# A four-layer graph network on one core: the attention's first tiles made in layer 2, its outer heads summed in float32, and layer 3's chunks run further ahead

## The chip, the cores and the metric

The program runs on one core of one Trainium2 chip. The metric is the device time of one execution in microseconds, as the median of several runs. The core's engines run beside each other and meet only at semaphores: TensorE (PE) multiplies matrices from SBUF into PSUM, PEld is its loading of weights, VectorE is called DVE, ScalarE ACT, GpSimd POOL, and SyncE (SP) issues most of the DMA transfers. Each engine executes its own queue in order, so an instruction that waits holds up all that stands behind it on that engine.

## The reference, cut to what matters

Four layers work on 2708 nodes with 512 features each and one adjacency matrix. Each layer normalizes its rows, takes the positive part, aggregates over neighbors and adds the result to its input. Layer 2 is the attention that the change is about (8 heads of 64 columns):

```python
Wh = jnp.einsum('nd,hdo->hno', x, W)
f1 = jnp.einsum('hno,ho->hn', Wh, a1)
f2 = jnp.einsum('hno,ho->hn', Wh, a2)
e = jax.nn.leaky_relu(f1[:, :, None] + f2[:, None, :], negative_slope=ALPHA)
e = jnp.where(adj[None, :, :] > 0, e, NEG_INF)
attention = jax.nn.softmax(e, axis=-1)
h_prime = jnp.einsum('hnm,hmo->hno', attention, Wh)
out = jax.nn.elu(h_prime)
```

Layer 3 averages the neighbors, multiplies by two weight matrices (fused with a third at the kernel's start) and takes the positive part.

## The kernel before, in words

Rows are cut into 22 chunks of 126 (the last has 62). Line numbers are those of the kernel before.

*Around the attention.* Layer 2 starts with a pass over its 22 chunks (`staged`, with one function per stage and a lag for each): load a chunk of x, normalize, transpose on PE (`hT_ps`), multiply by the attention's weights on PE (`wh_ps`, L182), copy, and write the product to the DRAM array `whd`. Beside it DVE and POOL form the two sums f1 and f2 of each head, PE transposes f1 into rows (`row2`, L728), which go to the DRAM array `rT`; the last four rows are done inside the attention.

*The attention* (from L829) never forms a softmax over raw scores. Since exp(leaky_relu(a + b)) is the larger of two products of factors of a and of b, a tile of weights needs one DVE instruction (`make`, L895): the larger of a broadcast row `rb` (factor of the node that asks) and a column `ec` (factor of the neighbor), times the 0/1 pattern of the adjacency `vT`. The rest of the neighbor's factor, `ef`, is multiplied into the neighbor's rows of `wh` by ACT (`scale`, L868, giving `whs`). The work goes unit by unit. A unit is a head over all 2708 nodes; the first and the last head are each cut into two units, over 1384 and 1324 nodes, so there are ten units: 2 halves, 6 full heads, 2 halves. Each unit takes 22 steps, one for each chunk of neighbors, 220 steps in all.

In each step `multiply` (L919) sends the tile through PE twice. The `av` product, with 64 columns of `whs`, works in quarters of the array's columns: four matmuls of 32 columns each run side by side on four parts of the tile. A float32 matmul appears in the trace as two passes. The `sums` product is the softmax's denominator. In 9 of 22 steps it is a float32 product with a further 32 columns of `whs`, made by a second ACT instruction (L870). In the 13 others, listed in `BY_SIDE`, ACT compares the tile against a threshold by a steep sigmoid (`compare`, L880, result `b` in bf16), and PE multiplies `b` in bf16 by the neighbor's factors split into three bf16 parts (`parts`); this gives a part of the denominator, and the remainder needs, for each node, the sum of the neighbor's factors over its neighbors. That is `count_neighbors`: for each of the 13 chunks, ACT turns the adjacency pattern into bf16 in four quarters (L978, `x<-vT`, in the five buffers named `x` that also hold chunks of x) and PE multiplies them by the parts (L983, `adj_sums`). Before, it stands behind steps 66 to 78, the first 13 of head 2 (unit 3, as heads and units count from 0). The parts are split by POOL in `exps2`.

At a unit's end ACT copies the sums out of PSUM (`evict`, L958) and SP writes them to the DRAM arrays `avT` and `sumT`. A list, `plan`, says behind which step each such thing is issued; a scheduler then places the instructions on the engines, and may place one ahead of its position in the program where it finds nothing that holds it. Up to four weight tiles exist at once (`TILES`), so DVE can be three steps ahead of PE. [...]

*After the attention* layer 3 passes over the chunks again. For each: load its part of `avT` and `sumT` (`load3`), transpose and divide on PE and DVE (`turn3`), apply elu on POOL, ACT and DVE (`elu3`), normalize, save x, transpose (`hT_ps`), and multiply by two weights (`nb_ps`, `self_ps`, L182). For the first chunks some of this is placed in the attention's last steps. Then comes layer 3's aggregation, 132 groups of products with the adjacency (L330), whose PE time ends the kernel.

Of the kernel before, what the change touches and what calls it, by code (L numbers as in the profile page):

```python
# [20 lines left out]
P = 128  # L21

R = 126
# [21 lines left out]
def fast_layers(  # L45
# [59 lines left out]
    KMAX = max(sizes)  # L105
    EARLY = NC // 2
# [152 lines left out]
    def load_x(src, c, name="x", pool=None, bufs=5, twice=False):  # L259
        n = rows(c)  # L260
        t = (pool or common).tile([P, D], F32, name=name, bufs=bufs)
        if twice and c == NC - 1:
            nc.gpsimd.memset(t[:R], 0.0)
            move(nc.sync, t[TAIL : TAIL + n, :], src[c * R : c * R + n, :])
        move(nc.sync, t[:n], src[c * R : c * R + n, :])
        return t
# [383 lines left out]
    l2 = ctx.enter_context(ExitStack())  # L650
    cp = l2.enter_context(tc.tile_pool(name="l2", bufs=1, side="right", reuse_waits="tile"))
# [5 lines left out]
    ef = cp.tile([R, NC, H], F32, name="ef")  # L657
    ec = cp.tile([R, NC, H], F32, name="ec")
    eb = cp.tile([R, NC, H], F32, name="eb")
    parts = cp.tile([R, NC * H * 8 + S], BF16, name="parts")  # L660
    nc.gpsimd.memset(parts, 0.0)
    parts_of = parts[:, : NC * H * 8].rearrange("p (m h k) -> p m h k", h=H, k=8)
    parts2 = cp.tile([R, NC, 3 * H], BF16, name="parts2")
    one6 = cp.tile([R, S], F32, name="one6")
    nc.gpsimd.memset(one6, 0.0)
    nc.gpsimd.memset(one6[:, 6:7], 1.0)
    row = {}

    def load_row1(h, lo, hi):

        if lo == 0:
            row[h] = cp.tile([R, N], F32, name="rb", bufs=2)
        src = rT[h : h + 1, lo:hi]
        nc.sync.dma_start(
            row[h][:, lo:hi],
            bass.AP(tensor=src.tensor, offset=src.offset, ap=[[0, R], [1, hi - lo]]),
        )

    def exp_row(h, lo, hi):
        t = row[h][:, lo:hi]  # L680
        nc.scalar.activation(t, t, AF.Exp, scale=1.0 - SLOPE2)

# [43 lines left out]
    def row2(c):  # L726
        pf = ps.tile([P, R], F32, name="f_ps", tag="ps")
        nc.tensor.transpose(pf[:H], f12[:R, c, :H], ident[:R, :R])  # L728
        r = cp.tile([H, R], F32, name="row", bufs=2)
# [3 lines left out]
    def exps2(cs):  # L733
        nc.scalar.activation(ef[:, cs], f12[:R, cs, H:], AF.Exp)
        nc.scalar.activation(ec[:, cs], f12[:R, cs, H:], AF.Exp, scale=SLOPE2 - 1.0)
        nc.gpsimd.tensor_scalar(eb[:, cs], ec[:, cs], -STEEP * ABOVE, None, op0=ALU.mult)
        size = cs.stop - cs.start
        rest = cp.tile([R, EARLY, H], F32, name="rest")[:, :size]
        for i, e in enumerate((ef, ec)):
            if i:  # L740
                nc.gpsimd.tensor_tensor(rest, ec[:, cs], ef[:, cs], ALU.mult)
                e = rest
            else:
                e = ef[:, cs]
            for k in range(3):
                part = parts_of[:, cs, :, 3 * i + k]
                nc.gpsimd.tensor_copy(part, e)
                if k < 2:
                    nc.gpsimd.tensor_tensor(rest, e, part, ALU.subtract)
                    e = rest  # L750
        nc.gpsimd.tensor_copy(
            parts2[:, cs].rearrange("p m (h k) -> p m h k", k=3), parts_of[:, cs, :, 3:6]
        )
# [4 lines left out]
    def rows2(c):  # L758
        if c < LATE:
            row2(c)  # L760
        if c == EARLY - 1:
            load_row1(*units[0])
        if c == NC - 4:
            exps2(slice(0, EARLY))
            exp_row(*units[0])

# [6 lines left out]

    ws = load_weight(weights, fused[0], "wfs", tag="w")
    wn = load_weight(weights, fused[1], "wfn", tag="w")
# [3 lines left out]
    e3 = e3_ctx.enter_context(tc.tile_pool(name="e3", bufs=2, reuse_waits="tile"))  # L779
    er = e3.tile([R, NC, H], F32, name="er", bufs=1)  # L780
    kept3 = {}
# [58 lines left out]
    with ExitStack() as stack:  # L840
        at = stack.enter_context(tc.tile_pool(name="att", bufs=1, reuse_waits="tile"))
        weight, wh, whs, acc, sides = {}, {}, {}, {}, {}
        steps = [(u, m) for u in range(len(units)) for m in range(NC)]


        GROUP = 3

        def load_wh(s):
            u, m = steps[s]
            h = units[u][0]  # L850
            t = at.tile([R, GROUP, O], F32, name="wh", bufs=3)
            k = min(GROUP, NC - 1 - m)
            if k > 0:
                src = whd[m * R : (m + k) * R, h * O : (h + 1) * O]
                nc.sync.dma_start(t[:, :k], src.rearrange("(k p) o -> p k o", p=R))
            if k < GROUP and m + k == NC - 1:
                src = whd[(NC - 1) * R :, h * O : (h + 1) * O]
                nc.sync.dma_start(t[:last_rows, k], src)
            for j in range(GROUP):
                wh[u, m + j] = t[:, j]  # L860

        def scale(s):

            u, m = steps[s]
            h, q = units[u][0], rows(m)
            t = at.tile([R, O + S], F32, name="whs", bufs=4)
            by = ef[:q, m, h : h + 1]
            nc.scalar.activation(t[:q, :O], wh.pop((u, m))[:q], AF.Copy, scale=by)  # L868
            if m not in BY_SIDE:
                nc.scalar.activation(t[:q, O:], one6[:q], AF.Copy, scale=by)  # L870
            whs[s] = t

        def compare(s):

            u, m = steps[s]
            h, lo, hi = units[u]
            q = rows(m)
            if m in BY_SIDE:
                b = at.tile([R, N], BF16, name="b", bufs=2)
                nc.scalar.activation(  # L880
                    b[:q, : hi - lo],
                    weight[s][:q, : hi - lo],
                    AF.Sigmoid,
                    bias=eb[:q, m, h : h + 1],
                    scale=STEEP,
                )
                sides[s] = b

        def make(s):
            u, m = steps[s]  # L890
            h, lo, hi = units[u]
            q = rows(m)
            g, k = where[m]
            t = at.tile([R, N], F32, name="t2", bufs=TILES)
            nc.vector.scalar_tensor_tensor(  # L895
                t[:q, : hi - lo],
                row[h][:q, lo:hi],
                ec[:q, m, h : h + 1],
                vT[g][:q, k, lo:hi],
                op0=ALU.max,  # L900
                op1=ALU.mult,
            )
            weight[s] = t

        def pieces(w):

            k = -(-w // 512)
            cuts = [round(i * w / k) for i in range(k + 1)]
            return list(zip(cuts, cuts[1:]))

        def sizes_of(u):
            _, lo, hi = units[u]
            return (hi - lo) // 2, (hi - lo) // 4

        def four(out, size, operands, m):

            for p, (a, b) in zip(out, pieces(size)):
                for j, (lhsT, rhs, part) in enumerate(operands):
                    nc.tensor.matmul(  # L919
                        p[j * S : j * S + lhsT.shape[1], : b - a],  # L920
                        lhsT,
                        rhs[:, part * size + a : part * size + b],
                        start=(m == 0),
                        stop=(m == NC - 1),
                    )

        def multiply(s):
            u, m = steps[s]
            q = rows(m)
            half, quarter = sizes_of(u)  # L930
            if m == 0:
# [847 lines left out]
```

## Time and profile before

| | us |
|---|---|
| median of 3 runs (range) | 1877.04 (1876.25 to 1879.04) |
| the profiled execution | 1876.26 |
| its span, first to last instruction | 1874.1 |
| PE busy in the span | 1803.5 (96%) |
| DVE busy | 1302.2 (69%) |
| ACT busy | 900.5 (48%) |
| POOL busy | 234.5 (13%) |
| mean granted clock of TensorE | 0.984 of full |

The busy times of engines overlap. A matmul's end is modelled, so a full PE row says that PE had work issued all the time, not that it ran at its peak. In the profile's lines L is the line of the kernel, the arrow reads "output from inputs", x is a count, and the bracket at a timeline row's end gives the idle time of that engine ahead of it and what ended it.

First starts of the attention's units on PE, read from the trace: 901.2, 941.1 (head 0), 974.4, 1039.7, 1128.1, 1192.8, 1257.8, 1323.3 (heads 1 to 6), 1388.5, 1421.9 (head 7); the last `av` matmul starts at 1456.2, layer 3's first product at 1473.5, and its aggregation at 1646.4.

### The profile page before, as it was taken

The numbers are of one execution on the slowest core, as the hardware profiler recorded it, in microseconds if no ns is written. First come the engines' busy times: TensorE is split into PE (matmuls) and PEld (weight loads), VectorE is DVE, ScalarE is ACT, GpSimd is POOL, SyncE is SP. The second block draws the span as 40 slices with busy tenths as digits, with TensorE's granted clock in tenths as the row PEclk, the third lists the DMA queues.
The fourth block names the chain that finished last, engine by engine and source line by source line (L and its number), as shares of the span: only waits on it lengthen the run. The fifth ranks groups of instructions, "written<-read, shape, count | busy, mean of one in ns | idle before, by whom it ended". The sixth has DMA issues, their size and how long they took to land.

```text
span 1874.1 us, 30317 instructions
## 1 busy us (share of the span) xinstructions
PE 1803.5 (96%) x11670; PEld 1057.0 (56%) x11670; DVE 1302.2 (69%) x1944; ACT 900.5 (48%) x1533; POOL 234.5 (13%) x219
## 2 busy tenths in 40 slices
PE   8999999989999999989899999999999799999998
PEld 4555677654447887744344443444444455478886
DVE  4655888874444566566899879999999766524333
ACT  2555887862220000056786897777777666400000
POOL 0000111211110122157400000000000222100000
PEclk9999999999999999999899999999999899999999
DMA  6423555542222112143320221210211444203321
GB/s 216 129 84 93 161 157 149 146 123 66 72 72 76 45 54 74 53 147 102 95 65 11 58 55 44 59 54 17 58 32 46 119 137 138 87 31 93 106 68 43
DMA packets 126037, 161.00 MB, mean 86 GB/s; under 512 B 57406, under 2 KB 77994, under 8 KB 125002
## 3 DMA queue, kind: packets, MB, share of 16 engines
q1 hardware_dynamic: 106764, 123.51, 23.2%
q10 hardware_dynamic: 18544, 33.37, 5.3%
q0 software_dynamic: 576, 2.10, 0.4%
q8 instruction: 94, 1.54, 0.3%
q14 instruction: 59, 0.48, 0.1%
HBM read 111.34 MB, written 47.42 MB: 85 GB/s over the span
## 4 chain that ended last, share of the span: by engine, by line
PE 65%; DVE 12%; issue 5%; ACT 4%; DMA 3%; POOL 0%; SPq 0%; DVEq 0%; ACTq 0%; POOLq 0%
PE acc L330 25%; PE av L919 12%; PE nb_ps L182 8%; DVE t L895 7%; PE self_ps L182 4%; PE line_ps L182 4%; PE sums L919 4%; PE wh_ps L182 4%; DVE cum L428 3%; PE hT_ps L210 2%; DMA rb<-rT 1%; DMA ai<-in_adj 1%; ACT cum L443 1%; ACT b L880 1%; ACT x L978 1%
## 5 line engine op out<-in xcount | busy, mean ns | idle before, releaser
L895 DVE SCALAR_TENSOR_TENSOR t<-rb,ec,vT 126x2708 f32<-126x2708 f32 (+2 forms) x220 | 528.2, 2470 | 25.5 <-ACT b L880 12.5
L919 PE MATMUL av<-t,whs 126*32 126x451 f32 (+4 forms) x4576 | 443.7, 517 | 8.7 <-ACT whs L868 7.5
L330 PE MATMUL acc<-halves,kt 126*126 126x512 f32 x1848 | 430.4, 394 | 1.2 <-DVE kt L1133 1.1
L330 PEld LDWEIGHTS acc<-halves,kt 126*126 126x126 f32 x1848 | 343.8, 186 | 85.4 <-DVE kt L593 1.5
L880 ACT ACTIVATE b<-t,eb 126x2708 bf16<-126x2708 f32 (+5 forms) x130 | 272.6, 2097 | 41.0 <-DVE t L895 40.2
L919 PEld LDWEIGHTS av<-t,whs 126*32 126x32 f32 (+1 forms) x4576 | 167.7, 110 | 204.1 <-issue 161.1
L330 PE MATMUL acc<-halves,ar 126*126 126x512 f32 x924 | 254.9, 415 | 6.1 <-ACT vT L483 4.9
L330 PEld LDWEIGHTS acc<-halves,ar 126*126 126x126 f32 x924 | 164.5, 188 | 50.9 <-issue 9.2
L593 DVE SCALAR_TENSOR_TENSOR kt<-lastr,index,vT 126x504 fp32r<-126x504 int16 (+1 forms) x132 | 105.0, 804 | 82.8 <-PE acc L330 82.8
L191 ACT ACTIVATE ln_rs<-ln_mv,eps 126x1 f32<-126x1 f32 x88 | 25.3, 293 | 276.9 <-DVE ln_mv L189 271.2
L1133 DVE CAST kt<-vT 126x504 fp32r<-126x504 int8 (+1 forms) x132 | 52.7, 400 | 140.8 <-PE acc L330 140.8
L428 DVE TENSOR_TENSOR_SCAN cum<-ai,deg 126x504 int16<-126x504 int32 (+2 forms) x110 | 126.1, 1157 | 34.4 <-DMA ai<-in_adj 19.5
L821 POOL TENSOR_SCALAR z<-y 126x512 f32<-126x512 f32 x22 | 43.0, 1956 | 648.3 <-DVE y L814 579.9
L443 ACT ACTIVATE cum<-cum,limit 126x504 int16<-126x504 int16 (+3 forms) x132 | 88.4, 670 | 65.4 <-DVE deg L436 63.4
L919 PE MATMUL sums<-t,whs 126*32 126x339 f32 (+3 forms) x1152 | 108.6, 454 | 4.6 <-ACT out L958 4.5
L868 ACT ACTIVATE whs<-wh,ef 126x64 f32<-126x64 f32 x220 | 73.8, 341 | 67.6 <-PE sums L919 34.7
L187 DVE BATCH_NORM_STATS2 ln_st<-x 126x6 f32<-126x512 f32 x88 | 60.4, 687 | 55.2 <-DMA x<-x 45.2
L212 ACT ACTIVATE hT<-hT_ps 128x504 f32<-128x504 f32 x88 | 51.4, 585 | 85.3 <-PE hT_ps L210 81.4
L483 ACT CAST vT<-vT_ps 126x504 int8<-126x504 f32 (+1 forms) x132 | 70.0, 536 | 27.4 <-DVE sums L474 17.8
L182 PE MATMUL wh_ps<-w2s,hT 128*126 128x512 f32 (+1 forms) x176 | 81.8, 609 | 0.0
L182 PE MATMUL h_ps<-w0s,hT 128*126 128x512 f32 x176 | 80.1, 598 | 0.9 <-ACT hT L212 0.9
L182 PE MATMUL nb_ps<-wn,hT 128*126 128x512 f32 x176 | 80.7, 601 | 0.0
(173 smaller groups left out, 2025.4 us busy)
## 6 DMA issues: line engine op xcount, KB each, us to landing
x<-x SPq DMA_DIRECT2D x105, 252.0 KB
x<-x ACTq DMA_DIRECT2D x84, 252.0 KB
ai<-in_adj SPq DMA_DIRECT2D x84, 249.0 KB
x<-in_x SPq DMA_DIRECT2D x42, 252.0 KB
rb<-rT SPq DMA_DIRECT2D x7, 1332.8 KB
wh<-whd SPq DMA_DIRECT2D x70, 94.5 KB
whd<-wh SPq DMA_DIRECT2D x21, 252.0 KB
aT<-avT SPq DMA_DIRECT2D x21, 252.0 KB
```

What stands on the lines that cost most here:

```text
L182: nc.tensor.matmul(po[:n], lhsT[:, f, :n], w[:, f, :], start=(f == 0), stop=(f == NF - 1))
L187: nc.vector.bn_stats(st[:n], xc[:n])
L330: nc.tensor.matmul(acc[:R], weight[:, k * R : (k + 1) * R], parts[:, i, :], start=(m == 0 and i == 0), stop=(m == NC - 1),)
L428: nc.vector.tensor_tensor_scan(cum[:n, :gw], ai[:n, :gw], ai[:n, :gw], 0.0 if g == 0 else deg[:n, m : m + 1], op0=ALU.add, op1=ALU.max,)
L443: nc.scalar.activation(cum[:n, :gw], cum[:n, :gw], AF.Sign, bias=limit[:n], scale=-1.0, accum_out=signs[:n, m, g : g + 1],)
L483: nc.scalar.copy(vT[g][:, :, m * R : (m + 1) * R], pt[:R, :K, :R])
L593: nc.vector.scalar_tensor_tensor(by_chunk(kt, cs), lastr[:, cs[0] * R : (cs[-1] + 1) * R].rearrange("p (c r) -> p c r", r=R), index[:R, m ...
L868: nc.scalar.activation(t[:q, :O], wh.pop((u, m))[:q], AF.Copy, scale=by)
L880: nc.scalar.activation(b[:q, : hi - lo], weight[s][:q, : hi - lo], AF.Sigmoid, bias=eb[:q, m, h : h + 1], scale=STEEP,)
L895: nc.vector.scalar_tensor_tensor(t[:q, : hi - lo], row[h][:q, lo:hi], ec[:q, m, h : h + 1], vT[g][:q, k, lo:hi], op0=ALU.max, op1=ALU.mult,)
L919: nc.tensor.matmul(p[j * S : j * S + lhsT.shape[1], : b - a], lhsT, rhs[:, part * size + a : part * size + b], start=(m == 0), stop=(m == ...
L1133: nc.vector.tensor_copy(by_chunk(kt, cs), pattern(m, cs))
```

## The change

- The attention's tiles and helper functions are set up ahead of layer 2's chunks. Behind its last three chunks stand `scale` and `make` of the first three steps, with the first loads of `wh` (`rows2`); the later ones follow three steps ahead of `multiply`, as before.
- `by_side` restricts the sigmoid and the bf16 sums to heads 1 to 6. Heads 0 and 7 (the four half units) take all their sums in float32.
- The casts of the adjacency (`mask`) and `count_neighbors` move from unit 3 to steps 11 to 37, in head 0, two casts a step. The splitting of the factors is done once for all chunks (`split`, behind step 9) by ACT and DVE instead of POOL.
- Layer 3's weights are loaded and the nodes' factor `er` made behind step 30.
- Layer 3's first chunks are placed in a new table near the end of the attention, and its loop is written by hand: product `nb3`, transpose of the next chunk, turn of the chunk three ahead, normalization two ahead, elu three ahead, load five ahead, then `self3`.
- The reductions of the final checks (`bad`) are issued behind the last chunk's sum. Some pools change sides of SBUF.

```diff
+    def by_side(u, m):
+        return 0 < units[u][0] < H - 1 and m in BY_SIDE
...
         if c == NC - 4:
             exps2(slice(0, EARLY))
             exp_row(*units[0])
+            load_wh(0)
+            load_wh(GROUP)
+        if c > NC - 4:
+            scale(len(made))
+            make(len(made))
...
-            if m not in BY_SIDE:
+        if not by_side(u, m):
...
+    def split():
+
+        nc.scalar.mul(eb, ec, -STEEP * ABOVE)
+        for i in range(2):
+            e = ef
+            if i:
+                nc.vector.tensor_tensor(rest, ec, ef, ALU.mult)
+                e = rest
+            for k in range(3):
+                part = parts_of[:, :, :, 3 * i + k]
+                nc.scalar.copy(part, e)
+                if k < 2:
+                    nc.vector.tensor_tensor(rest, e, part, ALU.subtract)
+                    e = rest
+        heads = slice(1, H - 1)
+        nc.scalar.copy(parts2[:, :, heads], parts_of[:, :, heads, 3:6])
...
+    def mask(i, j):
+        m = BY_SIDE[i]
+        q = rows(m)
+        g, k = where[m]
+        t = masks[i, j] = common.tile([P, D], F32, name="x", bufs=XBUFS).bitcast(BF16)
+        nc.scalar.copy(t[:q, :quarter], vT[g][:q, k, j * quarter : (j + 1) * quarter])
...
+    behind(9, split)
+    behind(30, load_l3_weights)
+    behind(30, exp_nodes)
...
-        for i in range(len(BY_SIDE)):
-            behind(3 * NC + i, count_neighbors, i)
+    for i in range(len(BY_SIDE)):
+        for j in range(4):
+            behind(11 + 2 * i + j // 2, mask, i, j)
+        behind(13 + 2 * i, count_neighbors, i)
...
-        end = len(steps)
-        for c in range(3):
-            behind(end - 14 + 2 * c, load3, c)
-            behind(end - 6 + 2 * c, turn3, c)
-        behind(end - 5, elu3, 0)
-        behind(end - 3, normalize3, 0)
-        behind(end - 3, elu3, 1)
+    for at_step, fn, c in (
+        (16, load3, 0),
+        (15, load3, 1),
+        (9, turn3, 0),
+        (8, load3, 2),
+        (8, elu3, 0),
+        (6, normalize3, 0),
+        (6, save3, 0),
+        (6, turn3, 1),
+        (5, load3, 3),
+        (2, transpose3, 0),
+        (2, turn3, 2),
+        (1, load3, 4),
+    ):
+        behind(len(steps) - at_step, fn, c)
...
-        stages = (
-            (0, load3, 3),
-            (1, turn3, 3),
-            (2, elu3, 2),
-            (3, normalize3, 1),
-            (4, save3, 0),
-            (4, transpose3, 0),
-            (5, multiply3, 0),
-        )
-        staged(NC, *((lag, skip(fn, first)) for lag, fn, first in stages))
+        elu3(1)
+        normalize3(1)
+        save3(1)
+        elu3(2)
+        for c in range(NC):
+            nb3(c)
+            if c:
+                do(transpose3, c + 1)
+            do(turn3, c + 3)
+            do(normalize3, c + 2)
+            do(save3, c + 2)
+            do(elu3, c + 3)
+            do(load3, c + 5)
+            final = self3(c)
+            if c == 0:
+                transpose3(1)
...
-        nc.vector.tensor_reduce(bad[:, 0:1], ind, AX.X, ALU.add)
+        with tc.issue_after(final):
+            nc.vector.tensor_reduce(bad[:, 0:1], ind, AX.X, ALU.add)
```

## The prediction

> **What bounds the kernel now.** I read the share of busy time first (PE 96%, everything else below 70%), then the chain of waits by line, then the busy time by stage with stage bounds set at TensorE's first matmul of each attention unit, and last the timeline at the two seams of the attention.
>
> ```profile
> core 0: us, PE busy (x) PEld busy (x) DVE busy (x) ACT busy (x) POOL busy (x), PEclk, DMA share, GB/s
> 893.20:901.20 8.00, 0.55 (x2) 0.00 (x0) 6.68 (x11) 1.85 (x7) 5.84 (x7) 0.67 0.67 184
> 901.20:974.40 73.20, 69.98 (x952) 30.95 (x952) 69.64 (x48) 63.87 (x108) 14.38 (x10) 0.97 0.23 61
> 974.40:1042.00 67.60, 67.48 (x796) 28.24 (x796) 67.60 (x23) 45.87 (x46) 0.00 (x0) 1.00 0.16 50
> 1042.00:1125.00 83.00, 75.11 (x828) 40.01 (x828) 64.66 (x23) 79.36 (x106) 0.00 (x0) 0.96 0.18 47
> 1191.00:1256.00 65.00, 64.92 (x780) 28.05 (x776) 65.00 (x23) 47.78 (x52) 0.00 (x0) 1.00 0.17 45
> 1456.20:1473.50 17.30, 5.49 (x33) 4.09 (x26) 13.49 (x36) 15.26 (x20) 6.51 (x4) 0.58 0.39 103
> 1473.50:1646.30 172.80, 171.74 (x537) 85.47 (x536) 107.67 (x267) 99.12 (x137) 35.01 (x20) 0.99 0.39 120
> ```
>
> The row at 1191 is a plain full-width head: 65 us for 22 steps, PE and DVE both full, ACT at 48. The row at 1042 is head 2, the one with the neighbor sums: 79.36 of 83 us are ACT's, DVE is down to 64.66. By first `av` matmuls the units last 65.3, 88.3, 64.7, 65.0, 65.5 and 65.1 us (heads 1 to 6), so head 2 costs 23.6 us more than its neighbor. The rows at 893 and 1456 are the seams: PE does 0.55 of 8 us and 5.5 of 17.3 us, and the granted clock falls to 0.67 and 0.58.
>
> The first seam (timeline, us of start and duration):
>
> ```profile
> 893.78 0.35 SPq L171 DMA_DIRECT2D wfn<-fused  x1
> 896.60 1.41 SPq L855 DMA_DIRECT2D wh<-whd  x3
> 900.82 0.83 ACT L868 ACTIVATE whs<-wh,ef 126x64 f32<-126x64 f32 x3 [2.21 <-DMA wh<-whd]
> 901.22 2.54 PE L919 MATMUL av<-t,whs 126*32 126x346 f32 x16 [7.46 <-ACT whs L868]
> 915.07 0.13 PEld L919 LDWEIGHTS av<-t,whs 126*32 126x32 f32 x4 [0.16 <-issue]
> 915.36 0.13 PEld L919 LDWEIGHTS av<-t,whs 126*32 126x32 f32 x4 [0.16 <-issue]
> ```
>
> SP's `wh` loads stand behind `wfn`, whose buffer is free only when the last layer-2 product is done; so PE waits 7.6 us (893.6 to 901.2). The last two rows are the pace of four column-tiled float32 passes over 346 columns: 0.292 us. A full-width head shows the other two prices:
>
> ```profile
> 1207.59 0.12 PEld L919 LDWEIGHTS <-parts 126*32 126x32 bf16 x4 [0.26 <-issue]
> 1207.73 0.28 PEld L919 LDWEIGHTS av<-t,whs 126*32 126x32 f32 x8
> 1208.26 0.13 PEld L919 LDWEIGHTS av<-t,whs 126*32 126x32 f32 x4 [0.25 <-issue]
> 1208.64 0.14 PEld L919 LDWEIGHTS av<-t,whs 126*32 126x32 f32 x4 [0.24 <-issue]
> ```
>
> Four bf16 matmuls over 338 columns take 0.14 us, a float32 pass over 451 columns 0.38 us (0.00084 us a column); a float32 product is two passes. The second seam:
>
> ```profile
> 1460.42 0.46 PE L919 MATMUL sums<-b,parts 62*32 62x331 bf16 x4 [3.79 <-ACT b L880]
> 1472.61 1.07 PE L210 MATMUL hT_ps<-ident,hn 126*128 126x126 f32 x4 [6.22 <-DVE ln_mv L189]
> 1473.48 4.94 PE L182 MATMUL nb_ps<-wfn,hT 128*126 128x512 f32 x8
> ```
>
> PE waits for the last sigmoid, then for chunk 1's norm; the first product, 3.44 us when warm, takes 4.94.
>
> **The change, part by part.** Since PE is full between the seams, I sum PE's time from the last layer-2 product on and ask at each stage whether DVE or ACT ends later.
>
> *Start.* Three tiles, their scaled `wh` and the `wh` loads move ahead of `wfn` and among the last layer-2 chunks; in the built order the first four tiles stand among DVE's last seven chunks. Cover: DVE is busy 61.7 of 91.2 us there, ACT 53.4, and the last batch-norm statistics are already behind, so 4 x 1.65 us of tiles (the mean of the first tiles) hit only the f sums, whose transposes PE needs two chunks (8 us) later. Without the cover it would be 6.6 us. On SP each of the three `wh` loads waits for stores of `whd` issued just ahead of it, and x loads stand behind it; these run two chunks ahead, 8 us, against the 4.1 us that the x load at 810 on the chain took. POOL gets one small memset, 0.5 us. Seam 7.6 to 0.3: **-7.3**.
>
> *Head 0.* Its 26 side steps lose a sigmoid (1.45 us of ACT) and get float32 sums. A half step becomes 4 x 0.292 + 2 x 0.292 = 1.75 us of PE, 1.68 at 331 columns, against 1.57 and 1.51 of DVE (spacing of the tiles): PE sets the pace. 22 x 1.75 + 22 x 1.68 = 75.5; the neighbor sums move in, 26 groups of four bf16 matmuls x 0.145 = 3.8; four row transposes about 0.4 each as seen at 906 to 912, 1.6. Sum 81 against 73.2: **+7.8**. ACT per two steps: two pairs of scales at 0.45 (1441.66 to 1442.11) and four casts at 0.65 (their spacing in head 2) = 3.5 us against PE's 3.8, so the casts hide. The split of the factors leaves POOL for ACT and DVE: seven copies and five subtractions or products of 176 columns, some 0.3 us each, 2 us of ACT and 1.5 of DVE ahead of the casts, hidden by PE's lead of 0.2 us a step on DVE and 1.3 on ACT. The row loads stay where they were in SP's queue.
>
> *Heads 1 to 6.* 414.0 us now. Head 2's 52 casts leave (52 x 0.65 = 34 us of ACT), and with them its 23.6 us, as do the waits of up to 4 us on late evictions there. DVE starts with three tiles in hand; PE's own work per head is 22 x 2.28 + 9 x 1.14 + 13 x 0.29 = 64.2, DVE's 22 x 2.95 = 64.9. I take 64.8 a head, 388.8: **-25.2** (-28.8 if PE alone sets it, -21 at the old 65.5).
>
> *Head 7 to layer 3's first product.* Now 1388.45 to 1473.48, 85.0 us. After: 38.5 for the first half, and 14 steps x 1.68 = 23.5 until chunk 0 is turned in the second (its loads go out seven steps earlier, 11.8 us; today's go out at 1429.5 behind the evictions and PE uses them at 1446.6 without a wait). Then DVE's chain for chunk 0: one tile ahead of it 1.6, the reciprocal 0.7, y 0.7, POOL's z 2.0, tanh, table load and exp 0.63 + 1.28 + 0.63, then elu, sum, statistics 2.3 with a tile between 1.6, load and root 1.6, the last tile, y of chunk 1, x and hn 3.9: hn is ready 16.4 us after the turn can start. PE arrives at its transpose after two turns (0.8 each, 1446.61 to 1447.41) and seven steps, 13.3: a wait of 3 us. Transpose, turn and the last step add 2.9: 19.3. Sum 81.3: **-3.7**. Here the Trainium skill ("ScalarE: Activation LUTs", What ACT_TABLE_LOAD costs) speaks against the change: a switch of tables costs 1.28 us of load and 1.38 us of drain. The load at 1455.73 takes 1.28 and its activation starts at 1457.03, so I see no drain, and take the row; with the page's drain on the chain's two switches hn comes 2.8 us later, and the part is worth -0.9. The page "TensorEngine Tiling (Array Packing)", Key Properties, lets each change of tiling mode drain TensorE; turns among the 32-column steps cost 0.80 here and 0.62 inside layer 3, so I price that at 0.18 a turn, already in the sum.
>
> *Layer 3's chunks.* Products and transposes are the same and PE runs 170.1 us without a gap from the first warm product to the last (22 x 6.87 + 17 turns x 0.62 + 20 transposes x 0.43 = 170.2, so nothing is left to win). Two turns and one transpose more now fall inside, 1.7; the second chunk's product stands right behind its own transpose and waits 0.9 for ACT's copy. The checks `bad` now come behind the last sum, and the verdict matmul ahead of the aggregation's first: two reductions 0.94, five small ones 0.7: 1.7 later. The old seam was 1.25 and the cold first product 1.5. 172.9 to 175.6: **+2.7**. Float32 tiles of the ring move to the attention's side; all its readers are done by then.
>
> *Aggregation*: 227.8 us, unchanged.
>
> Sum: -7.3 + 7.8 - 25.2 - 3.7 + 2.7 = **-25.7**. The profiled run took 1876.26 us for a span of 1874.1, the median is 1877.04; so span about 1848, and **1851 us**.
>
> **The rivals.**
> 1. *PE's floor.* No DVE limit in heads 1 to 6 (-3.6), no wait for hn (-3), none at the verdict: 1842. For it: PE did head 1 to 6 work without gaps. Against: DVE's tiles follow each other without a gap too.
> 2. *The second seam stays.* If chunk 0's chain is 6 us later than I have it, PE idles for more than the 4.2 us that cost it the clock at 1042, and loses some 10 us: 1861. For it: POOL's z took 2.76 at 1452 beside a running tile.
> 3. *The first tiles don't come early*, since the scales or the row wait behind something in the layer-2 chunks: 7.6 us stay, 1859. The built order speaks against it.
> 4. *Slower: the casts bind head 0.* Five buffers, four to a count, so three casts start only when the previous count is done. If they bind as they did in head 2 (23.6 / 13 = 1.8 us a round), the gain is gone but for 2 us; it turns slower from 25.7 / 13 = 2.0 us a round, and with 2.4 us a round it ends at 1882. For it: the same casts did this before. Against: ACT had 2.54 us sigmoids beside them then, and needs 3.5 us for a round of 3.8 now.
>
> **How the numbers follow.** My own case 0.66, with a range of 1845 to 1857; rival 1: 0.12; rival 2: 0.11; rival 3: 0.05; rival 4: 0.06, 0.04 of it past the point where it decides. The range of 1842 to 1863 takes in rivals 1 to 3 and the ends of the unknown costs. This kernel's runs tell 0.2% (3.8 us) from no change: faster 0.95, same 0.01, slower 0.04.
>
> **What would show it.** Right: PE without a gap over 1 us at the first seam and clock 1.0 there; head 0 near 81 us with PE full; head 2 as long as head 4; a wait of 2 to 4 us for hn near the end; layer 3 starting near 1445. Wrong: PE waiting for `x` casts in head 0, PE waiting for ACT's scales there, a gap over 4 us at layer 3's start, or a full head that takes longer than 66 us although nothing was added to it.

## The result, and the profile after

The changed kernel takes 1867.61 us (median of 4 runs, 1864.1 to 1870.72), the kernel before 1876.64 us beside it: 0.995 of the time, with a 95% interval of 0.9928 to 0.9971. So it is faster, by 9 us where 25.7 were forecast, and the time lies above the range of 1842 to 1863. Its profiled execution took 1866.35 us for a span of 1864.5.

The span of both profiles, cut at the same events on PE (first layer-2 product, last one's end, first `av` matmul of a unit, layer 3's first product, the first matmul of its aggregation, the end), in us. The last column is the kernel with five edits of the experiments below (its profiled execution took 1847.8 us, 4 us less than its median):

| stage | before | after | change | forecast | five edits |
|---|---|---|---|---|---|
| to layer 2's first product | 801.98 | 802.53 | +0.5 | 0 | 799.21 |
| layer 2's products | 91.77 | 94.66 | +2.9 | 0 | 91.59 |
| seam to the attention | 7.46 | -0.07 | -7.5 | -7.3 | -0.07 |
| head 0 | 73.22 | 81.17 | +7.9 | +7.8 | 81.16 |
| heads 1 to 6 | 414.02 | 394.73 | -19.3 | -25.2 | 387.98 |
| head 7, to layer 3's first product | 85.03 | 82.10 | -2.9 | -3.7 | 82.11 |
| layer 3's chunks | 172.87 | 179.84 | +7.0 | +2.7 | 175.49 |
| aggregation | 227.76 | 229.50 | +1.7 | 0 | 228.55 |
| span | 1874.11 | 1864.47 | -9.6 | -25.7 | 1846.02 |

The first row varies from run to run: in the profiles of all kernels told of here it lies between 799.0 and 802.5.

The stage view of the changed kernel, with the same columns as in the prediction (stretch, length, busy time of five engines with counts of instructions, granted clock, DMA share, GB/s):

```profile
core 0: us, PE busy (x) PEld busy (x) DVE busy (x) ACT busy (x) POOL busy (x), PEclk, DMA share, GB/s
802.50:897.20 94.70, 91.33 (x280) 42.59 (x282) 68.97 (x165) 55.12 (x119) 55.07 (x46) 0.96 0.41 126
...
875.80:880.50 4.70, 4.70 (x11) 2.57 (x12) 4.70 (x5) 3.43 (x6) 2.00 (x1) 0.65 0.02 4
...
897.10:978.30 81.20, 81.20 (x1166) 36.76 (x1166) 73.76 (x54) 67.07 (x163) 2.49 (x2) 1.00 0.31 90
...
1042.40:1110.60 68.20, 65.02 (x784) 29.50 (x782) 68.20 (x24) 47.66 (x52) 0.00 (x0) 1.00 0.18 51
...
1176.50:1241.50 65.00, 64.91 (x780) 27.50 (x776) 64.97 (x23) 47.69 (x53) 0.00 (x0) 1.00 0.17 45
...
1455.10:1635.00 179.90, 174.03 (x557) 86.64 (x553) 125.77 (x295) 104.78 (x145) 40.08 (x23) 0.99 0.42 124
```

The row at 897 is head 0: PE is busy from end to end, and ACT, with 47 of the 52 casts (the scheduler placed five ahead, in layer 2), has 14 us to spare. The row at 1042 is head 2. Its ACT time has fallen to 47.66 us, as in head 4 at 1176, yet it takes 3.2 us longer than head 4, and PE lacks just those 3.2. By first `av` matmuls heads 1 to 6 take 64.1, 68.1, 66.0, 65.0, 65.0 and 66.5 us. The missing gain lies in three places, each of which the timeline shows by what PE waited for. The first is in layer 2, 24 us ahead of the seam (start, duration; in brackets the idle time of the engine and what ended it):

```profile
868.67 1.66 DVE L724 SCALAR_TENSOR_TENSOR t<-rb,ec,vT 126x1384 f32<-126x1384 f32 x1 [0.97 <-ACT rb L688]
...
870.25 1.76 DVE L766 TENSOR_TENSOR wh_a<-wh,arow 126x512 f32<-126x512 f32 x1
...
872.86 1.64 DVE L724 SCALAR_TENSOR_TENSOR t<-rb,ec,vT 126x1384 f32<-126x1384 f32 x1
873.84 1.78 POOL L766 TENSOR_TENSOR wh_a<-wh,arow 126x512 f32<-126x512 f32 x1 [1.24 <-ACT wh L761]
874.42 1.23 DVE L785 TENSOR_SCALAR f<-f 126x16 f32<-126x16 f32 x1
...
875.80 0.37 PE L796 MATMUL f_ps<-ident,f 126*8 126x126 f32 x1 [2.71 <-DVE f L785]
...
897.13 1.37 PE L908 MATMUL av<-t,whs 126*32 126x346 f32 x16
```

Two early tiles add up here. The first (868.67) stands ahead of DVE's product for f, which then runs into POOL's and takes 1.76 us where it took 0.69 a chunk before; so the sums of f are done at 872.93, 1.5 us late (chunks follow each other every 3.97 us, and the last sums were done at 867.45). The second stands between these sums and their clamp, L785, which starts another 1.5 us late and takes 1.23 us instead of 0.2. PE's transpose of f stands ahead of the next product, so PE waits 2.71 us, and the row at 875 above shows a clock of 0.65 for the 4.7 us after it. The seam itself is closed: `av` starts as the last product ends.

The second is the seam from head 1 to head 2:

```profile
1041.00 1.28 ACT L688 ACT_TABLE_LOAD   x1
1044.73 2.46 ACT L688 ACTIVATE rb<-rb 126x2708 f32<-126x2708 f32 x1 [2.44 <-DMA rb<-rT]
...
1047.54 1.38 ACT L947 COPY out<-av 128x451 f32<-128x451 f32 x3
1048.11 1.35 PE L908 MATMUL sums<-t,whs 126*32 126x338 f32 x16 [3.18 <-ACT out L947]
```

PE's first denominators of head 2 wait for the copies of head 1's sums out of PSUM; a full head holds five of the eight buffers of the kernel's PSUM pool, so two heads don't fit. The copies stand on ACT behind the exponential of head 3's row (two short scales are between), and that waits for the row's transfer, issued at 1038.35 when DVE had read the old row for the last time. The same order at the next seams cost 1.03 us (head 3) and 1.61 us (head 6).

The third is around layer 3's start and end:

```profile
1452.16 0.62 PE L211 MATMUL hT_ps<-ident,hn 126*128 126x126 f32 x4 [1.83 <-DVE hn L202]
...
1462.71 0.59 PE L211 MATMUL hT_ps<-ident,hn 126*128 126x126 f32 x4
1462.88 1.71 POOL L875 TENSOR_SCALAR z<-y 126x512 f32<-126x512 f32 x1 [6.37 <-DVE y L868]
1464.63 0.63 ACT L878 ACTIVATE th<-z 126x512 f32<-126x512 f32 x1 [2.53 <-POOL z L875]
...
1465.83 0.57 ACT L213 ACTIVATE hT<-hT_ps 128x504 f32<-128x504 f32 x1
1466.45 5.25 PE L183 MATMUL nb_ps<-wfn,hT 128*126 128x512 f32 x8 [3.15 <-ACT hT L213]
...
1634.85 0.19 PE L1150 MATMUL verdict_ps<-bad,ones 128*1 128x2 f32 x2 [2.72 <-DVE bad L1148]
```

Chunk 1's transpose was ready at 1463.3, but ACT's copy of it stands behind the tanh and exp of a later chunk, which wait for POOL. The product then takes 5.25 us, against the 3.6 us of later chunks.

### The profile page after: what moved, and what is told of

The parts are those of the page before. It is cut to its first block, busy times and chain, and to the rows that moved or that the text cites. A ratio compares the mean times of both kernels' runs of the same rounds, so it can differ in the third digit from the quotient of the medians.

```text
span 1864.5 us, 30673 instructions
## 1 busy us (share of the span) xinstructions
PE 1808.8 (97%) x11878; PEld 1053.9 (57%) x11878; DVE 1315.9 (71%) x1949; ACT 843.1 (45%) x1536; POOL 214.6 (12%) x194
## 4 chain that ended last, share of the span: by engine, by line
PE 62%; DVE 16%; issue 5%; DMA 4%; ACT 2%; POOL 1%; DVEq 0%; SPq 0%; ACTq 0%; POOLq 0%
PE acc L331 27%; DVE t L724 10%; PE av L908 8%; PE nb_ps L183 8%; PE line_ps L183 4%; PE sums L908 4%; PE self_ps L183 4%; PE wh_ps L183 3%; DVE cum L429 3%; DMA rb<-rT 2%; PE hT_ps L211 1%; DMA x<-x 1%; DMA ai<-in_adj 1%; PE vT_ps L472 1%; ACT cum L444 1%
## 5 line engine op out<-in xcount | busy, mean ns | idle before, releaser
L908 PE MATMUL av<-t,whs 126*32 126x451 f32 (+3 forms) x4576 | 434.7, 513 | 0.6 <-DVE ln_mv L190 0.6
L908 PEld LDWEIGHTS av<-t,whs 126*32 126x32 f32 (+1 forms) x4576 | 161.7, 110 | 203.8 <-issue 179.8
L742 ACT ACTIVATE b<-t,eb 126x2708 bf16<-126x2708 f32 (+1 forms) x78 | 199.0, 2551 | 22.1 <-DVE t L724 22.0
L908 PE MATMUL sums<-t,whs 126*32 126x338 f32 (+5 forms) x1568 | 139.1, 448 | 6.0 <-ACT out L947 5.8
L908 PEld LDWEIGHTS sums<-t,whs 126*32 126x32 f32 (+1 forms) x1568 | 55.3, 109 | 73.6 <-issue 37.7
L183 PE MATMUL nb_ps<-wfn,hT 128*126 128x512 f32 x176 | 80.9, 603 | 3.1 <-ACT hT L213 3.1
L484 ACT CAST vT<-vT_ps 126x504 int8<-126x504 f32 (+1 forms) x132 | 69.9, 535 | 26.6 <-DVE sums L475 17.1
```

The lines of the kernel that those rows point to most:

```text
L183: nc.tensor.matmul(po[:n], lhsT[:, f, :n], w[:, f, :], start=(f == 0), stop=(f == NF - 1))
L484: nc.scalar.copy(vT[g][:, :, m * R : (m + 1) * R], pt[:R, :K, :R])
L742: nc.scalar.activation(b[:q, : hi - lo], weight[s][:q, : hi - lo], AF.Sigmoid, bias=eb[:q, m, h : h + 1], scale=STEEP,)
L908: nc.tensor.matmul(p[j * S : (j + 1) * S, : b - a], lhsT, rhs[:, part * size + a : part * size + b], start=(s % NC == 0), stop=(s % NC == ...
```

## The experiments

The theory after the traces: the forecast's rates are right, and the gap of 16 us is made of separate waits, each put there by the place of one instruction in an in-order queue. The rival: PE, DVE and ACT are near their limits together, so that a wait taken away comes back as another. Each edit below is made to the changed kernel unless said otherwise. The intervals of most single edits overlap with that of the changed kernel (0.9928 to 0.9971), so a single edit is judged by its stage in the profile, and the time decides on the five together.

**The early tiles behind the clamps.**

```diff
-            make(len(made))
+            with tc.issue_after(clamped[14 + len(made)]):
+                make(len(made))
```

> The changed kernel, with one edit: each early tile of head 0 stands on DVE behind the clamp of f that the next row transpose needs, one chunk of layer 2 later than in the changed kernel. Theory: in the changed kernel the second early tile stands between the sums of f and their clamp, and PE waits 2.71 us for that clamp and then runs at half clock for some 4 us; from layer 2's first product to the end of its last it takes 94.7 us against 91.8 before. Then that stretch goes back to 91.8 to 92.3, the seam to the attention stays closed (under 0.5 us), and the kernel is 2.5 to 3 us shorter. Rival: the stretch is the mere extra work on DVE and ACT beside POOL, in whatever order; then it stays above 94, or the seam opens by what is won.

Measured: 1863.8 us (0.9943 of before, 0.9925 to 0.9961); layer 2's products 91.65 us, the seam still -0.07. Timeline of this kernel:

```profile
872.08 0.21 DVE L785 TENSOR_SCALAR f<-f 126x16 f32<-126x16 f32 x1
872.20 1.65 DVE L724 SCALAR_TENSOR_TENSOR t<-rb,ec,vT 126x1384 f32<-126x1384 f32 x1
873.55 0.27 PE L797 MATMUL f_ps<-ident,f 126*8 126x126 f32 x1
...
882.82 0.27 PE L797 MATMUL f_ps<-ident,f 126*8 126x126 f32 x1 [1.16 <-DVE f L785]
```

`clamped` keeps the clamp instructions of the chunks. The same tile right behind the clamp costs nothing; two tiles in one chunk still cost 1.16 us, without a fall of the clock. Most of the loss was the order, not the amount of work. Head 7 took 84.18 us here against 82.10, since the clock fell behind its wait for `hn`; the last section says when it does.

**The exponential later.** `scaled` keeps ACT's scale instructions.

```diff
+            elif fn is exp_row and s > 2 * NC:
+                with tc.issue_after(scaled[s]):
+                    fn(*args)
```

> The changed kernel, with one edit: from head 2 on, the exponential of the next head's row stands on ACT behind the scale of a later step (some ten steps into the unit) instead of at the unit's seam. Theory: in the changed kernel PE's three gaps in heads 2, 3 and 6 (3.18, 1.03 and 1.61 us) come from this exponential, which waits 6.3 to 7.9 us for its row's transfer at the head of ACT's queue, with the next scale and the first evictions behind it. Then the gaps go, heads 1 to 6 take 389 to 390 us instead of 394.7, and the kernel is 5 us shorter. Rival: the gaps belong to the evictions themselves or to PE running out of tiles, whatever stands on ACT; then heads 1 to 6 stay within 1 us of 394.7.

Measured: 1863.17 us (0.9937, 0.9912 to 0.9961). Heads 1 to 6 took 391.86 us: heads 3 and 6 fell to 65.1, but head 2 only to 67.4. Half the theory held. What was left at head 2's seam, in this kernel:

```profile
1042.15 2.55 ACT L743 ACTIVATE b<-t,eb 126x2708 bf16<-126x2708 f32 x1 [2.87 <-DVE t L725]
1044.61 1.39 ACT L948 COPY out<-av 128x451 f32<-128x451 f32 x3
1045.18 1.35 PE L909 MATMUL sums<-t,whs 126*32 126x338 f32 x16 [2.41 <-ACT out L948]
```

With the exponential gone, the new head's first sigmoid stands ahead of the copies and waits for its tile.

**The sigmoid behind the copies**, on top of the last edit:

```diff
+            if copied and (s + 1) % NC == 1:
+                with tc.issue_after(copied[-1]):
+                    compare(s + 1)
+            else:
+                compare(s + 1)
```

> The kernel with the later exponential, with one edit more: at the seam of two full heads the first sigmoid of the new head stands on ACT behind the three copies of the old head's sums, not ahead of them. Theory: what is left of the loss in heads 1 to 6 (a gap of 2.41 us at head 2's seam, 391.9 us in all) is this sigmoid: it waits for its tile, then takes 2.55 us, and PE's first denominators of the new head wait for the bank that the copies free. Elsewhere it costs nothing since PE runs 7.3 us behind DVE; at head 2's seam it is 4.2 us behind. Then the gap falls below 0.8 us, and heads 1 to 6 take 389.3 to 390.3 us. Rival: PE would meet the end of DVE's lead anyway; then the gap only moves into the head and the sum stays at 391.5 or more.

Measured: 1860.7 us (0.9908, 0.9886 to 0.9929). Heads 1 to 6: 64.1, 64.7, 64.7, 64.7, 64.8 and 64.9 us, in sum 387.98, without a gap of PE above 0.6 us. In this kernel, at the same seam:

```profile
1042.50 1.01 ACT L948 COPY out<-av 128x451 f32<-128x451 f32 x2
...
1045.40 2.55 ACT L743 ACTIVATE b<-t,eb 126x2708 bf16<-126x2708 f32 x1 [0.89 <-DVE t L725]
1045.90 1.33 PE L909 MATMUL sums<-t,whs 126*32 126x338 f32 x16
```

The first two copies are done 2 us before PE needs the banks. So the 5.9 us missing in heads 1 to 6, and 0.8 more, were ACT's order at the seams. The rival of this run (PE meets the end of DVE's lead anyway) is out. Layer 2 took 96.06 us in this profile, with a second gap of 2.21 us at the next chunk's clamp, though neither edit touches that stage.

**The same two edits in the kernel before**, to see whether its gap of 3.69 us at head 2's seam was the exponential's as well:

> The kernel before, with the two edits on ACT alone: the later exponential from head 2 on, and the first sigmoid of a full head behind the copies of the old head's sums. Theory: the gap of 3.69 us at head 2's seam in the kernel before was the exponential's wait too, and not the casts'; it goes, with the half clock behind it, and head 2 falls from 88.3 to 82 to 85 us; the gap of 3.74 us at head 2's end, behind the copies of the neighbor sums, stays; the kernel is 3 to 5 us shorter than before. Rival: the casts bind ACT through all of head 2, so what is won at its seam is lost again within the head; then head 2 stays at 87 or more.

Measured: 1874.18 us against 1876.12 (0.9988, 0.998 to 0.9997). The rival held. Heads 4 to 6 gained (64.7 us each, where they took 65.0, 65.5 and 65.1), but head 2 rose from 88.3 to 92.9 us. In this kernel, some 11 us into head 2:

```profile
1045.70 2.55 ACT L883 ACTIVATE b<-t,eb 126x2708 bf16<-126x2708 f32 x1 [2.44 <-DVE t L898]
1048.15 2.06 ACT L983 CAST x<-vT 126x677 bf16<-126x677 int8 x3
1048.94 0.30 PE L988 MATMUL adj_sums<-x,parts 126*24 126x338 bf16 x1 [3.12 <-ACT x L983]
```

The gap at the seam is gone, but within the head PE waits for casts, for 4.75 us in all where it was 0.41. The casts of this row stand behind a sigmoid, and for its tile ACT had idled 2.44 us: again the order of ACT's queue. All waits of PE in head 2 are 1.3 us longer than before, and the clock was at half for 10.2 us where it was for 6.8, worth some 1.7 us. That is 3 us of the 4.6 that head 2 lost; the rest stays open. So beside the casts the seam's order gained nothing in head 2, and the other heads gained 1.6 us.

**The casts back in head 2**, and nothing else:

```diff
-            behind(11 + 2 * i + j // 2, mask, i, j)
-        behind(13 + 2 * i, count_neighbors, i)
+            behind(3 * NC + i - 1, mask, i, j)
+        behind(3 * NC + i, count_neighbors, i)
```

> The changed kernel with one part undone: the casts of the adjacency and the neighbor sums stand in head 2 again, from one step ahead of its first step on; all else is as in the changed kernel. Theory (the prediction's terms of 3.8 us for the sums in head 0 and 23.6 us for the casts in head 2): head 0 falls from 81.2 to 77 to 78 us, head 2 rises from 68.1 to 86 to 92, and the kernel is 15 to 20 us longer than the changed one. Rival: the casts' price of before came from POOL's splitting and the rest of head 0's end, and with five buffers and three tiles in hand they now mostly hide; then head 2 takes under 76 us.

Measured: 1885.92 us (1.0041 of before, 1.0028 to 1.0055), some 18 to 21 us above the changed kernel. Head 0 fell to 77.18 us, head 2 rose to 85.3, with ACT busy for 80.53 of them. The 4 us of neighbor sums in head 0 are as forecast. Head 2 is 17.1 us longer than in the changed kernel, a little less than the theory had and well under the 23.6 us of the prediction; PE's wait for the copies at its seam is there in both kernels (3.02 and 3.18 us), but here the clock was at half for 6.8 us behind it and there it was not; without that the casts would be worth less still. Another 4.2 us of the difference are head 4's, which lost 2.81 us to the same kind of wait and then the clock (0.73 over the next 6 us). This part carries more than the whole gain: without it the change is slower than before.

**Chunk 1's transpose and copy first.**

```diff
             nb3(c)
             if c:
                 do(transpose3, c + 1)
+            else:
+                final = self3(c)
+                transpose3(1)
             do(turn3, c + 3)
...
-            final = self3(c)
-            if c == 0:
-                transpose3(1)
+            if c:
+                final = self3(c)
```

> The changed kernel, with one edit: in layer 3's loop, for chunk 0 alone, the self product and the transpose of chunk 1 stand ahead of the turn and elu of chunk 3. Theory: in the changed kernel PE waits 3.15 us for chunk 1's transposed rows because ACT's copy of them stands behind the tanh and exp of a later chunk, which wait for POOL, and the half clock after it costs 1.7 to 2 us more; chunk 1's first product comes 11.3 us and chunk 2's a further 9.5 us later, where later chunks take 7.9. Then the gap is under 1 us, these two distances are 8 to 8.8 us, and the kernel is 4 to 5 us shorter. Rival: chunk 1's own normalization is late; then a gap of 2 us or more stays ahead of its transpose or its product.

Measured: 1864.82 us (0.9944, 0.9927 to 0.996). The first two distances between products are 8.24 and 8.01 us instead of 11.32 and 9.56. In this kernel:

```profile
1462.16 0.59 PE L211 MATMUL hT_ps<-ident,hn 126*128 126x126 f32 x4
...
1462.79 0.59 ACT L213 ACTIVATE hT<-hT_ps 128x504 f32<-128x504 f32 x1 [1.98 <-PE hT_ps L211]
...
1463.44 3.70 PE L183 MATMUL nb_ps<-wfn,hT 128*126 128x512 f32 x8
```

The copy follows its transpose at once. A wait of the rival's kind does come up, for another chunk: at 1475 PE waits 1.70 us for chunk 2's normalization, so layer 3's chunks came to 177.10 us, 2.7 less than in the changed kernel and not 4 to 5. The gap ahead of the aggregation was still there.

**The checks free**: `issue_after(final)` removed from the reductions `bad`.

> The changed kernel, with one edit: the reductions of the final checks are no longer held behind the last chunk's sum. Theory: PE waits 2.72 us for them ahead of the aggregation's first product, where the kernel before waited 1.1; the gap falls to 1.1 to 1.3 us, and the kernel is 1.5 us shorter. Rival: the gap is the weight tiles of the aggregation, which stand behind the same sum; then it stays above 2 us.

Measured: 1868.2 us (0.9962, 0.9948 to 0.9977). The gap ahead of the aggregation fell from 2.72 to 1.11 us, and PE then waits for the aggregation's first weight tile. So the theory holds for this wait. The median shows nothing of it, and why is open: the profiled execution was the fastest of the five (1863.12 us), and the other four have no trace. Even in it head 2 took 71.1 us, 3 us more than in the changed kernel, with nearly the same gap at its seam (3.23 us). Rows of the stage view in stretches of 3.41 us, the first two of this kernel, the last two of the changed one:

```profile
1042.60:1046.00 3.40, 0.76 (x8) 0.00 (x0) 3.40 (x3) 2.80 (x3) 0.00 (x0) 1.00 0.00 0
1046.01:1049.41 3.40, 2.83 (x24) 0.73 (x24) 2.80 (x2) 3.37 (x7) 0.00 (x0) 0.50 0.56 126
...
1042.95:1046.36 3.41, 1.98 (x24) 0.42 (x16) 3.41 (x2) 1.63 (x1) 0.00 (x0) 1.00 0.26 107
1046.36:1049.77 3.41, 1.66 (x24) 0.54 (x24) 3.41 (x2) 3.39 (x8) 0.00 (x0) 1.00 0.27 61
```

Here 2.64 us of the gap lie in one stretch, and the next has half clock; in the changed kernel the gap is split, 1.43 and 1.75 us, and the clock stays. The last section tells why the stretches were cut at these places. The same happened to head 7 in the run with the tiles behind the clamps: there the 1.83 us wait for `hn` was followed by 0.56, in the changed kernel by 1.00.

**All five edits, beside the changed kernel on the same chip.**

> The changed kernel with all five edits: the early tiles behind the clamps, the later exponential, the sigmoid behind the evictions, chunk 1's transpose and copy first, the checks free. Theory (each of the four places of loss is a wait of its own): layer 2 91.8, seam under 0.5, head 0 81.2, heads 1 to 6 389.3 to 390.3, layer 3's first distances 8 to 8.3 us, the gap ahead of the aggregation 1.1; in sum 13 us under the changed kernel, 1853 to 1856 us. Rival: waits that the edits take away come back as others (for DVE in head 0, for chunk 2's normalization) or as half clock behind the gaps that stay; then 1858 or more.

> The changed kernel once more, beside the five edits on the same chip. Theory: 1864 to 1870 us, with the stages as in its first profile, PE gaps of 2.7, 3.2, 1.0, 1.6, 1.8, 3.1 and 2.7 us at the same places, and a granted clock of half behind some of them, not the same ones as in the first profile. Rival: the clock falls at the same gaps each time.

Measured: five edits 1851.81 us (0.9862, 0.9841 to 0.9883), the changed kernel 1865.04 us (0.9931, 0.9916 to 0.9945). Stage rows of the kernel with five edits (layer 2, head 2, layer 3's chunks):

```profile
799.20:890.80 91.60, 89.57 (x280) 41.71 (x282) 67.31 (x165) 55.23 (x119) 58.77 (x46) 0.98 0.44 131
...
1036.10:1100.80 64.70, 64.70 (x784) 27.76 (x783) 64.70 (x23) 47.55 (x52) 0.00 (x0) 1.00 0.15 43
...
1442.00:1617.50 175.50, 172.63 (x557) 85.94 (x553) 122.39 (x290) 102.04 (x142) 39.78 (x23) 1.00 0.43 126
```

The waits were separate: what the edits win adds up (13 us were expected, 13.2 measured beside each other), and this version beats both kernels. Four gaps of more than 1 us are left from layer 2's first product on (1.16, 1.82, 1.69, 1.11), none followed by a fallen clock in either of its two profiles. Both profiles are of fast executions (1847.8 and 1847.94 us); what made others of this kernel take up to 1855.43 us is not shown. In its second profile the changed kernel had its gaps where it had them before, with half clock behind the same two of them (0.75 behind 2.71 and behind 3.15). For these two profiles the rival held, but other kernels with the same gaps had the fall elsewhere, as shown.

**A sixth edit: chunk 0's chain two steps earlier** (turn, elu, normalization and save of chunk 0 and the loads of chunks 0 to 2 in the table near the attention's end), beside the five once more.

> The kernel with the five edits and a sixth: in the attention's last steps chunk 0 of layer 3 is loaded, turned, passed through elu and normalized two steps (3.4 us) earlier. Theory: the 1.82 us for which PE waits for hn and the 0.6 us for a tile just ahead of it come from the length of chunk 0's chain after its turn, and not from its loads; then both fall below 0.5 us, and head 7 takes 79.8 to 80.5 us instead of 82.1. Rival: the loads, which follow the first half's evictions, are then late, or DVE's tiles are late by as much; then head 7 stays above 81.5.

> The kernel with the five edits once more, beside the sixth on the same chip. Theory: 1848 to 1855 us, stages within 0.5 us of its first profile but for the half clock behind the gaps of 1.82 and 1.69 us, which may or may not fall; each such fall costs 1.5 to 2.5 us. Rival: the first profile was a lucky one and the median is 1857 or more.

Measured: six edits 1848.37 us (0.9862, 0.9845 to 0.9878), five 1850.05 us (0.987, 0.9849 to 0.9891): no difference that these runs can tell. In the profile head 7 fell from 82.10 to 81.15 us, 1 us instead of the 2 expected and between the theory's range and the rival's: the wait for `hn` is gone, but PE now waits 0.91 us at layer 3's first product.

## Why the prediction was wrong

The direction and the part that carries it, the casts out of head 2, were right; the size was not. Of the forecast's own signs of being wrong one came true: heads 2 and 6 took more than 66 us (68.1 and 66.5). Point by point, with what each missed:

1. *Start* (3 us missed, leaving out the first row of the table). The seam closed as forecast, from 7.5 us to nothing. The step that failed is "4 x 1.65 us of tiles hit only the f sums, whose transposes PE needs two chunks (8 us) later". In the undisturbed chunk just ahead the clamp ends at 867.70 and PE's transpose starts at 868.95: the cover was 1.25 us, and the two tiles with what they pushed into POOL's work made the clamp's result 4.0 us late. DVE was busy for two thirds of that stage, and the forecast took the share of free time for slack, where the distance from producer to consumer had to be read.
2. *Head 0*: right, 81.17 us for 81. PE sets the pace, and the casts hide. Rival 4 is out.
3. *Heads 1 to 6* (5.9 us missed). The rate of 64.8 us a head was right, as 387.98 us for 388.8 shows once the seams are clear. The step that failed is "with them its 23.6 us, as do the waits of up to 4 us on late evictions there". The casts were worth 17.1 us at most in head 2, and the waits did not leave with them: in the changed kernel those at the seams of heads 2, 3 and 6 came to 5.8 us. The trace of before shows the same wait:

```profile
1042.49 2.46 ACT L681 ACTIVATE rb<-rb 126x2708 f32<-126x2708 f32 x1 [2.28 <-DMA rb<-rT]
...
1045.31 1.38 ACT L958 COPY out<-av 128x451 f32<-128x451 f32 x3
...
1045.88 2.31 PE L919 MATMUL sums<-t,whs 126*32 126x338 f32 x16 [3.69 <-ACT out L958]
```

It names ACT's copy as what ended the wait; further up ACT's queue stood the exponential, waiting for its row. The wait is there with the casts and without them; beside them, taking it away gained nothing in head 2.

4. *Head 7* (0.8 missed): two turns and a wait for `hn` as forecast; the wait was 1.83 us and not 3, with 0.58 us for a tile ahead of it. (The terms of the forecast's chain add up to 16.9 us and not to 16.4, which would make the wait 3.6.) That the table switch costs its load alone was right here too: in the changed kernel the load at 1049.19 starts 0.02 us behind the end of the instruction ahead of it, lasts 1.28 us, and its sigmoid starts 0.01 us later. The 1.38 us of drain of the Trainium skill's page "ScalarE: Activation LUTs" (What ACT_TABLE_LOAD costs) do not appear.
5. *Layer 3's chunks* (4.3 missed). The step is "the second chunk's product stands right behind its own transpose and waits 0.9 for ACT's copy": the copy also waited for what stood ahead of it on ACT. PE's wait came to 3.15 us, 2.2 more than that, and the half clock behind it cost 1.6 (chunk 2's product came 9.56 us behind chunk 1's; with the checks free, where the clock held behind the same wait, 8.01). That is 3.8 of the 4.3 us. The checks were priced rightly: from the last product to the aggregation's first it took 2.84 us instead of 1.23, 1.6 more, where 1.7 was forecast.
6. *Aggregation* (1.7 missed). Its matmuls took 0.7 us more and what follows them 1.1. In the other profiles of kernels with the change the 0.7 is there too (2.2 in three of them, where the clock fell just ahead), and the part behind the last matmul varies from 8.7 to 9.7 us. The cause stays open.

Rival 2 was near in kind: layer 3's start lost 5 us to a gap with half clock behind it, but by chunk 1's copy and not by chunk 0's chain. (The gap at 1042 from which that rival took its threshold lasted 3.69 us, not 4.2, and gaps of half that length can cost the clock.)

The forecast is near the kernel in which these instructions stand elsewhere in their queues: 1851 us, where the five edits give 1851.81 and 1850.05. Part of this is chance. Heads 1 to 6 agree for the forecast's reason (388.0 for 388.8). Layer 3's 175.5 for 175.6 does not: a wait of 1.69 us for chunk 2's `hn`, which the forecast lacks, stands in for the 1.7 us of checks, which the five edits took away. And the five edits' profile has a span of 1846.0 us where about 1848 was forecast, mostly by what lies ahead of layer 2. What the forecast left out has one sign, since a wait can only add; the range should have been wider upward.

## What to carry to other kernels

When the busiest instructions leave an engine, look at what waits stood beside them in its queue, since these cost nothing until then; and follow the wait's releaser up its own queue, to what that engine was waiting for. For an instruction put among others, measure the cover as the time from the end of the result it delays to the start of its reader, not as a share of idle time. Where a transfer must land first, issue the instruction that uses it some steps into the next phase and not at its seam, where copies that free banks stand behind it.

## What the runs showed of the hardware that was not expected

*A short gap costs the clock or not by where it falls.* In the eleven profiles of kernels with the change there are, from layer 2's first product to the aggregation, 42 gaps of PE of 1.8 to 3.3 us. Behind 20 of them the mean granted clock of the next 6 us was 0.50 to 0.75, behind the others 1.00; behind 21 gaps of 0.85 to 1.70 us it was always 1.00. The same wait of 1.83 us for `hn` had 1.00 in seven profiles and 0.56 to 0.62 in three.

It looks like chance, but the traces show an order. In each profile the granted clock changes only on a grid with a step of 3.413 us (to within 0.003 us), and the grid lies elsewhere in each. In these eleven profiles and this part of the kernel there are 2651 windows of the grid at full clock. In 17 of them PE was idle for 1.94 us or more, and each was followed by a window at half clock; with up to 1.77 us idle none of 2627 was; of the 7 between (1.82 to 1.89 us) three were. These are all the 20 falls; in the two profiles of the kernel before and its variant, 8 of 8 windows with 1.94 us or more were followed by half clock, and no other. So a gap costs the clock when more than some 1.9 us of it lie in one window, and the rows at 1042 and 1046 above, cut at the grid of each profile, are one case of each kind.

The Trainium skill's page "TensorE: Matmul & The Clock Gate", What's actually happening, has a window of 3413 ns that runs free of the program, and lets the clock fall after an idle one. The step and the free phase are what these traces show; that a window need not be idle throughout is where they differ from the page, and the measurement decides.

A fall cost 1.6 us where the half clock lasted one window (9.56 for 8.01 in layer 3, above) and 3.0 us where it lasted two (head 2 of 71.1 for 68.1). For pricing, an estimate from these numbers: a gap of up to 1.8 us costs its own length. A gap of 2.7 us that falls anywhere on the grid has 1.9 us or more in one window with a chance of (3.41 + 2.7 - 3.8) / 3.41 = 0.68, and then costs 1.6 to 3 us more; of the 14 gaps of 2.70 to 2.72 us, 9 lost the clock.

*DVE's short clamp waits for POOL.* The clamp of 874.42 took 1.23 us, against 0.16 beside an idle POOL (at 880.76), and ended at 875.65, 0.03 us behind the end of POOL's product (873.84 + 1.78). In ten earlier chunks of the same profile the clamp met POOL's addition, took 0.53 us and ended 0.03 us behind it each time. That fits the lock of which the Trainium skill's page "SBUF — State Buffer", section SBUF: two separate sides, speaks: one of the two engines holds the shared ports for its whole instruction, and the other waits. So 1 us of the 2.71 us gap in layer 2 was not the early tiles' own length, but where they had pushed the clamp to.
